# Ten products of a constant tile ahead of the first layer's cumulative sum, and dt's columns copied ahead of the SiLUs

## The chip, the cores and the metric

The kernel runs as one program on one core of one Trainium2 chip. The metric is the time of one execution on the device, in microseconds. The time before is the median of three runs: 20413.0 us (20402.2 to 20426.97).

## The reference

A network of two "metaformer" layers works on x, 8 images of 128 channels and 64 x 64 positions (4096 tokens an image), in float32. Layer 0 is a four-direction selective scan and a layer of 64 experts; it isn't touched. Layer 1's token mixer is what the change touches. It is a state-space model ("SSD") that is applied in three places:

```python
def _mamba(x, in_w, in_b, conv_w, conv_b, A_log, D, dt_bias, rms_w, out_w, headdim, d_state):
    zxbcdt = x @ in_w.T + in_b
    z, xBC = zxbcdt[..., :di], zxbcdt[..., di:2 * di + 2 * d_state]
    dt = softplus(zxbcdt[..., -nh:] + dt_bias)
    xBC = silu(causal_conv_of_3(xBC, conv_w) + conv_b)
    xs, Bm, Cm = xBC[..., :di], xBC[..., di:di + d_state], xBC[..., di + d_state:]
    y = _ssd(xs * dt, dt * -exp(A_log), Bm, Cm) + D * xs
    y = y * silu(z)
    return (y * rsqrt(mean(y * y) + 1e-5) * rms_w) @ out_w.T

# in the mixer of layer 1
gf  = _mamba(gf, sm_...) + gf                      # the seeds: 8 channels, all images
def cascade(xi):                                   # for each of 8 splits of 16 channels
    for i in range(2):
        xi = _mamba(xi, cm_in_w[i], ...)           # 4 heads of 8, state of 64
    return xi
ys = vmap(cascade)(xs) + xs * skip_scale
```

_ssd is the chunked form of the recurrence: within a chunk, decays exp(cs[l] - cs[s]) of the cumulative sum cs of dt * A weigh the products C[l]·B[s]; across chunks a state is carried.

## The kernel before, in words

The second half of the program has three stages one after another: the seeds (function seeds), the cascade (cascade), and a last stage with the layer's convolutions and experts (second_ffn). The names in the profile end in _sm for the seeds and in _cm for the cascade.

The cascade cuts each image into 16 segments of 256 tokens, 128 segments in all, and handles all 8 channel splits of a segment at once. A segment passes through both _mamba layers. In each of them it is *projected* (ssd_project), worked on in two *chunks* of 128 tokens (ssd_chunk) and put out (ssd_output). The loop `for n in range(total + 2)` has 130 turns. A turn interleaves by hand four chunks (both of segment n in layer 0, both of segment n - 2 in layer 1), the projection of segment n + 1 in layer 0, the projection of segment n - 1 in layer 1, and the outputs. The functions are generators; each yield is a place where the loop may go on with another one. The order thus written is the order in which instructions are given out; a scheduler settles the order on each engine[...].

A projection makes, in this order:
- bc_p: B and C, on TensorE, then one SiLU on ScalarE for each bank pair;
- z_p: z, and its SiLU;
- tok_p: x, B and dt with the tokens on the partitions, once for each of the two chunks. A bank pair holds both halves of a chunk's columns. For each half, ScalarE takes the SiLU of the first columns (tok_cm, row L284) and VectorE copies dt's 16 columns (dtr_cm, row L993);
- silus_done: a table load on ScalarE, behind all SiLUs, for exp and ln;
- dt by softplus: Abs, Exp and Ln on ScalarE (e_cm, e_cm, dt_cm), maximum, products and sums on VectorE (r_cm, tmp_cm, dt_cm), and dA = dt * A on VectorE;
- ssd_exponents: the cumulative sum cs_p on TensorE, which waits for dA; its three bf16 parts on VectorE (csq_cm, csr_cm), sent to memory and back as rows of the exponents by SyncE's transfers (cs_cm, ssA_cm, ssB_cm, csw_cm, eA_cm);
- dec_p and cd_p: the decays to a chunk's end, on TensorE, each with an Exp on ScalarE.

A chunk has g_p (C·B, TensorE) and gm_cm (its mask, VectorE), pad_cm, xw_cm and xD_cm (x with dt, with the decay and with D; the last on GpSimd), ss_p (the exponents, eight TensorE products of 512 columns), E_cm (their Exp, on ScalarE, then times gm on VectorE, row L332), yo_s_p (the state's part), S_cm (the new state; Sd_cm, its copy, on GpSimd), y_p (the sum, many small TensorE products), yy_cm and yz_cm. An output has sq_cm, o_p and rs_cm.

PSUM is given out in rings: tag "a" has 3 pairs of banks in the cascade (bc_p, z_p, tok_p, g_p, ss_p), tag "b" has 2 banks (cs_p, dec_p, cd_p, yo_s_p, y_p, o_p). A tile in a ring waits for the readers of the tile that had its place.

The seeds run the same ssd_project, ssd_chunk and ssd_output for 16 segments (all images at once), interleaved with the preparation of their inputs, and end each segment with det_p, eight TensorE products that wait for gf on VectorE.

ssd_weights makes the constants of one such layer: called for the cascade's layers 0 and 1 and for the seeds with index 0 (second_setup). mm, act, tt and ts (rows L281, L284, L323, L326 to L329) are the helpers that issue one instruction each, so many groups of the profile share a line and are told apart by the tiles.

Of the kernel before, what the change touches and what calls it, by code (L numbers as in the profile page):

```python
# [9 lines left out]
F32 = mybir.dt.float32  # L10
BF16 = mybir.dt.bfloat16
AF = mybir.ActivationFunctionType
# [11 lines left out]
S = 512  # L24
# [247 lines left out]
class Net:  # L272
# [6 lines left out]

    def mm(self, out, lhsT, rhs, start=True, stop=True):  # L280
        self.ordered(self.nc.tensor.matmul(out, lhsT=lhsT, rhs=rhs, start=start, stop=stop))  # L281

    def act(self, out, in_, func, **kw):
        i = self.ordered(self.nc.scalar.activation(out, in_, func, **kw))  # L284
# [562 lines left out]
    def ssd_weights(self, pool, cfg, j):  # L847

        nc = self.nc
        n = f"{cfg.name}{j}"  # L850

        def part(i):
            o, m = self.at["stacked"][f"{n}_{i}"]
            return self.st[:, o : o + m]

        W = pool.tile([128, cfg.cols], F32, name=f"W_{n}")
        nc.vector.memset(W[96:], 0.0)
        self.tt(W[:KST], part(0), part(1), ALU.mult)
        self.tt(W[:KST], W[:KST], part(2), ALU.add)
        negA = pool.tile([128, cfg.nh], F32, name=f"negA_{n}")  # L860
        self.act(negA, self.w(f"{n}_Alog"), AF.Exp)
        self.ts(negA, negA, -1.0, ALU.mult)
        D = pool.tile([128, cfg.g2, cfg.nh, cfg.hd], F32, name=f"D_{n}")
        for g in range(cfg.g2):
            nc.vector.tensor_copy(D[:, g], bc(self.w(f"{n}_D"), cfg.hd))
        wo = pool.tile([cfg.pz, cfg.gh * cfg.co], F32, name=f"wo_{n}")
        self.ts(wo, self.w(f"{n}_out")[: cfg.pz], self.w(f"{n}_rms")[: cfg.pz], ALU.mult)
        return {"W": W, "negA": negA, "D": D.rearrange("p g h q -> p (g h q)"), "wo": wo}

    def ssd_rings(self, pool, cfg, n, npads, nrows, nstates):  # L870

# [33 lines left out]
        ring[what] = (q + 1) % len(ring[what + "s"])  # L905
        return ring[what + "s"][q]

    def ssd_exponents(self, cfg, dA, n_tok, ring, wk, ps):


        nc = self.nc
        NC, nh, G = n_tok // 128, cfg.nh, cfg.g
        n = NC * G * nh
        t_ = cfg.name
        p = ps.tile([128, S], F32, tag="b", bufs=self.narrow, name="cs_p")
        p = p[:n, :128]
        self.mm(p, dA.rearrange("p c g -> p (c g)"), self.k("le"))
        part = wk.tile([n, 3, 128], BF16, name=f"csq_{t_}")
        rest = wk.tile([n, 128], F32, name=f"csr_{t_}")
        whole = wk.tile([n, 128], F32, name=f"csw_{t_}")  # L920
        nc.scalar.copy(whole, p)
        nc.vector.tensor_copy(part[:, 0], p)
        self.tt(rest, p, part[:, 0], ALU.subtract)
        nc.vector.tensor_copy(part[:, 1], rest)
        self.tt(part[:, 2], rest, part[:, 1], ALU.subtract)
        d = self.dp.tile([3, n, 128], BF16, name=f"cs_{t_}", bufs=3)
        nc.sync.dma_start(d.rearrange("i n t -> n i t"), part)
        A, B = self.turn(ring, "row")
        g4 = cfg.g4
        for r in range(g4):  # L930
            v = d.rearrange("i (c g h) t -> i c g h t", g=g4, h=nh)[:, :, r]
            nc.sync.dma_start(B[32 * r : 32 * r + 3], v)
            for i in range(3):
                o = 32 * r + 3 + i * nh
                nc.sync.dma_start(A[o : o + nh, :, r], v[i].rearrange("c h t -> h c t"))
        w = self.dp.tile([n, 128], F32, name=f"csw_{t_}", bufs=3)
        nc.sync.dma_start(w, whole)
        NH, m = cfg.nhalf, cfg.gh * nh
        eA = wk.tile([cfg.pz, NH, n_tok], F32, name=f"eA_{t_}", bufs=4 if cfg is CM else 3)
        for c in range(NC):  # L940
            for hf in range(NH):
                at = (c * NH + hf) * m
                nc.sync.dma_start(eA[:, hf, c * 128 : (c + 1) * 128], bc(w[at : at + m], cfg.hd, 1))
        return A, B, eA

    def ssd_project(self, cfg, W, ring, stk, n_tok, wk, ps):
# [3 lines left out]
        nc = self.nc  # L950
        NP, G, nh, hd, hi, ds = cfg.np, cfg.g, cfg.nh, cfg.hd, cfg.hi, cfg.ds
        g2, NH, gh, pb, pz = cfg.g2, cfg.nhalf, cfg.gh, cfg.pb, cfg.pz
        GH = G * nh
        NC = n_tok // 128
        t_ = cfg.name
# [8 lines left out]
        for j0 in range(0, NP, per):  # L964
            p = ps.tile([128, 2, S], F32, tag="a", bufs=self.wide, name="bc_p")
            v = p.rearrange("p a s -> p (a s)")[:pb, : per * 2 * n_tok].rearrange("p (j x s) -> p j x s", x=2, s=n_tok)
# [15 lines left out]
        nbk, ppb = NP // cfg.ppb, cfg.ppb  # L982
        for c in range(NC):
            p = ps.tile([128, 2, S], F32, tag="a", bufs=self.wide, name="tok_p")
            for j in range(NP):
                o = (j % ppb) * cfg.wtok
                self.mm(p[:, j // ppb, o : o + cfg.wtok], stk(j)[:, c * 128 : (c + 1) * 128],
                        Wp[:, cfg.o_t : cfg.o_t + cfg.wtok])
            for q in range(nbk):
                v = p[:, q, : ppb * cfg.wtok].rearrange("p (j f) -> p j f", j=ppb)  # L990
                jj = slice(q * ppb, (q + 1) * ppb)
                silus.append(self.act(tok[:, c, jj, :], v[:, :, : cfg.wsil], AF.Silu))
                nc.vector.tensor_copy(dtr[:, c, jj, :], v[:, :, cfg.wsil :])  # L993
            if c < NC - 1:
                yield None
        self.silus_done(silus)
        yield "silu"


        def small(name, bufs=2):  # L1000
            return wk.tile([128, NC, GH], F32, name=f"{name}_{t_}", bufs=bufs)

        dtr = dtr.rearrange("p c j f -> p c (j f)")
        e, r, tmp, dA = (small(n) for n in ("e", "r", "tmp", "dA"))
        dt, w = (small(n, nl_) for n in ("dt", "wd"))
        self.act(e, dtr, AF.Abs)
        self.ts(r, dtr, 0.0, ALU.max)
        self.softplus(dt, r, e, tmp, nc.vector)
        self.tt(dA.rearrange("p c (g h) -> p (c g) h", h=nh), dt.rearrange("p c (g h) -> p (c g) h", h=nh),
                bc(W["negA"], NC * G, 1), ALU.mult)  # L1010
        yield None
        ssA, ssB, eA = self.ssd_exponents(cfg, dA, n_tok, ring, wk, ps)
        yield None

        p = ps.tile([128, S], F32, tag="b", bufs=self.narrow, name="dec_p")
# [651 lines left out]
    def run(self, ctx):  # L1667
        tc, nc, nb = self.tc, self.nc, self.nb
        cp = ctx.enter_context(tc.tile_pool(name="cp", bufs=1))
        dp = ctx.enter_context(tc.tile_pool(name="dp", bufs=1, space=DRAM))  # L1670
        self.kt = cp.tile(list(self.A["const"].shape), F32, name="kt")
        nc.sync.dma_start(self.kt, self.A["const"])
        self.xs = [dp.tile([C, L], F32, name=f"xs_{b}") for b in range(nb)]
        self.ys = [dp.tile([C, L], F32, name=f"ys_{b}") for b in range(nb)]
        self.x1 = [dp.tile([C, L], F32, name=f"x1_{b}") for b in range(nb)]
        self.x2 = [dp.tile([C, L], F32, name=f"x2_{b}") for b in range(nb)]
        self.seed = [dp.tile([C, L], F32, name=f"seed_{b}") for b in range(nb)]
        self.P = [dp.tile([NE, L], F32, name=f"P_{b}") for b in range(nb)]
        self.dp = dp
        self.eo = cp.tile([NE, nb, C], F32, name="eo")  # L1680
        with tc.tile_pool(name="mid", bufs=1) as mp:
            self.pooled = mp.tile([C, NE, nb], F32, name="pooled")
            with tc.tile_pool(name="l0", bufs=1) as pl:
                self.scan_weights(pl)
                self.silus_done([])
                r = pl.tile([C, L], F32, name="r")
                for b in range(nb + 1):
                    with tc.tile_pool(name=f"in{b}", bufs=1) as rp, tc.tile_pool(name=f"inw{b}", bufs=2) as wk, \
                            tc.tile_pool(name=f"inps{b}", bufs=1, space=PSUM) as ps:
                        gens = []  # L1690
                        if b:
                            gens.append(self.route_tokens(b - 1, r, rp, wk, ps))
                        if b < nb:
                            xp, xt = (pl.tile([C, L + 2 * PAD], F32, name=n) for n in ("xp", "xt"))
                            gens.append(self.scan_inputs(b, r, xp, xt, wk, ps))
                        self.turns(*gens)
                    if b < nb:
                        self.first_mixer(b, r, xp, xt)
            self.experts()
        self.act_fence = self.act_exp = None  # L1700
        pl = ctx.enter_context(tc.tile_pool(name="l1", bufs=1))
        self.weights(pl, "second")
        with tc.tile_pool(name="l1s", bufs=1, space=PSUM) as ps:
            self.second_setup(pl, ps)
        self.seeds()
        with tc.tile_pool(name="l1b", bufs=4, space=PSUM) as ps:
            self.gms = pl.tile([C, nb, NSC], F32, name="gms")
            self.wide, self.narrow = 3, 2
            self.cascade(ps)
        self.second_ffn()  # L1710
# [23 lines left out]
```

## Time and profile before

| what | value |
|---|---|
| median of three runs | 20413.0 us (20402.2 to 20426.97) |
| the profiled execution, its own time | 20402.59 us |
| its span, first to last instruction | 20400.8 us |
| mean granted TensorE clock | 0.913 |
| busy: TensorE, its weight loads, VectorE, ScalarE, GpSimd | 80%, 40%, 76%, 55%, 41% |
| seeds, about 9930 to 10900 us: TensorE busy, clock | 754 of 970 us, 0.75 |
| cascade, about 10900 to 18800 us: TensorE busy, clock | 6815 of 7900 us, 0.91 |
| cascade: cs_p, waits for dA | 519.5 us in 113 of them, between 11000 and 18000 us |

A row of a view in order of time gives the start and the length in us, engine, line, operation, the tile written and the tiles read, the shapes and how many instructions the row holds; in brackets the idle time of the engine just before it and whom it waited for. A shape such as 128*64 before the operand of a product says how much of the 128 x 128 array it fills, rows by columns. A row of waits names who waited, for whom, for how long in total, how often and at most. PEclk in the line of slices is the granted TensorE clock in tenths.

### The profile page before, as it was taken

Reading aid. Unit: us, or ns where it says so; the run is one execution under the profiler, and the core shown is the slowest. Engines: PE = TensorE matmul, PEld = TensorE weight load, DVE = VectorE, ACT = ScalarE, POOL = GpSimd, SP = SyncE. Lnnn points to the kernel's source line nnn. Section 1 sums busy time; section 2 is a strip of 40 time slices with the busy share of each in tenths; the row PEclk is TensorE's granted clock in tenths of the full one; section 3 lists DMA queues with packets and bytes.
Section 4 is the critical chain, followed back from the end, with each engine's and each line's share of the span. In section 5 each row is a group of like instructions: output and inputs, shape, how many; then the busy total and the mean of one; then the engine's idle time right before and its main releaser. Section 6 shows DMA issues by size and latency. Waiting matters only on the chain. (4 is left out here: it accounts for less than half of the span.)

```text
span 20400.8 us, 305956 instructions
## 1 busy us (share of the span) xinstructions
PE 16385.0 (80%) x115485; PEld 8172.9 (40%) x115485; DVE 15587.1 (76%) x21096; ACT 11132.5 (55%) x15963; POOL 8451.5 (41%) x6020
## 2 busy tenths in 40 slices
PE   6777777777777777777877888888888888888899
PEld 2222222222222222223534555555555555555343
DVE  7989899898989989897454666666666666666886
ACT  5555555555555555554344555555555555555553
POOL 6767677686767767675110111111111111111444
PEclk9999899899989999998777999999999999998899
DMA  4445454454545445454431111111111111111222
GB/s 117 136 110 137 109 134 132 111 138 109 136 107 134 139 110 135 112 133 118 150 122 37 36 35 36 35 36 36 35 36 36 35 35 36 36 35 40 80 97 80
DMA packets 991471, 1764.26 MB, mean 86 GB/s; under 512 B 202091, under 2 KB 590603, under 8 KB 981067
## 3 DMA queue, kind: packets, MB, share of 16 engines
q1 hardware_dynamic: 989998, 1744.68, 30.6%
q8 instruction: 917, 15.02, 0.3%
q14 instruction: 556, 4.55, 0.1%
HBM read 1511.36 MB, written 232.91 MB: 86 GB/s over the span
## 5 line engine op out<-in xcount | busy, mean ns | idle before, releaser
L323 POOL TENSOR_TENSOR bx<-xE,B 128x1024 f32<-128x1024 f32 x2048 | 4823.6, 2356 | 1420.3 <-DMA xE<-dtx_d 1316.1
L281 PE MATMUL dA<-parts,expand 128*128 128x512 bf16 x12288 | 3194.7, 398 | 2076.4 <-DVE last L335 1525.7
L284 ACT ACTIVATE dA<-dA,negA 128x1024 f32<-128x1024 f32 x2048 | 2228.6, 1088 | 3665.1 <-PE dA L281 3627.7
L615 DVE TENSOR_TENSOR_SCAN dA<-dA,last,bx 128x1024 f32<-128x1024 f32 x1536 | 3610.7, 2351 | 172.5 <-POOL bx L323 165.1
L281 PEld LDWEIGHTS <-expand 128*128 128x128 bf16 x12288 | 1073.4, 100 | 4799.9 <-DVE last L335 2710.5
L332 DVE SCALAR_TENSOR_TENSOR E_cm<-E_cm,gm_cm 128x1024 f32<-128x1024 f32 x2048 | 2418.8, 1217 | 741.9 <-ACT E_cm L284 741.7
L284 ACT ACTIVATE E_cm<-ss_p 128x1024 f32<-128x1024 f32 x2048 | 1959.8, 1027 | 1139.2 <-PE ss_p L281 1137.8
L323 DVE TENSOR_TENSOR hc<-dA,C 128x1024 f32<-128x1024 f32 x2048 | 2508.4, 1225 | 70.0
L1128 POOL COPY Sd_cm<-S_cm 64x128 f32<-64x128 f32 x1024 | 331.7, 324 | 4528.5 <-DVE S_cm L323 4418.8
L323 POOL TENSOR_TENSOR xD_cm<-tok_cm,D_cm 128x256 f32<-128x256 f32 x512 | 525.4, 1026 | 2591.9 <-PE y_p L281 1865.0
L281 PE MATMUL y_p<-E_cm,pad_cm 128*32 128x128 f32 x32768 | 1338.2, 276 | 45.2 <-DVE E_cm L332 44.9
L615 DVE TENSOR_TENSOR_SCAN dA<-dA,bx 128x1024 f32<-128x1024 f32 x512 | 1173.2, 2291 | 187.6 <-POOL bx L323 186.2
L281 PE MATMUL ss_p<-ssB_cm,ssA_cm 128*128 128x512 bf16 x4096 | 1297.9, 430 | 22.8 <-DMA ssB_cm<-cs_cm 10.8
L281 PE MATMUL y<-hc,kt 128*32 128x512 f32 x8192 | 1187.7, 645 | 29.3 <-DVE hc L323 29.3
L281 PEld LDWEIGHTS y_p<-E_cm,pad_cm 128*32 128x32 f32 x32768 | 964.9, 110 | 290.4 <-DVE E_cm L332 180.6
L281 PE MATMUL bc_p<-stk_cm,W_cm 128*128 128x256 f32 x4096 | 1026.0, 394 | 47.8 <-DMA stk_cm<-xs 20.6
L281 PEld LDWEIGHTS bc_p<-stk_cm,W_cm 128*128 128x128 f32 x4096 | 740.6, 191 | 264.4 <-issue 97.8
L323 DVE TENSOR_TENSOR gm_cm<-g_p,kt 128x1024 f32<-128x1024 f32 x512 | 623.7, 1218 | 256.0 <-PE g_p L281 256.0
L284 ACT ACTIVATE tok_cm<-tok_p 128x384 f32<-128x384 f32 x1024 | 502.8, 491 | 538.6 <-PE tok_p L281 397.4
L281 PE MATMUL g_p<-BC_cm 64*128 64x128 f32 x8192 | 729.7, 296 | 83.0 <-ACT BC_cm L284 51.1
L281 PE MATMUL tok_p<-W_cm,stk_cm 128*128 128x200 f32 x4096 | 767.8, 341 | 0.0
L332 DVE SCALAR_TENSOR_TENSOR dw<-h,w_second,dw 128x512 f32<-128x512 f32 x1024 | 723.3, 748 | 1.5 <-ACT h L284 1.2
(388 smaller groups left out, 29223.5 us busy)
## 6 DMA issues: line engine op xcount, KB each, us to landing
xE<-dtx_d SPq DMA_DIRECT2D x2048, 512.0 KB
dtx_d<-dtx SPq DMA_DIRECT2D x256, 256.0 KB
eA_cm<-csw_cm SPq DMA_DIRECT2D x1024, 64.0 KB
pb<-p_d SPq DMA_DIRECT2D x64, 1024.0 KB
x<-x SPq DMA_DIRECT2D x192, 256.0 KB
ssA_cm<-cs_cm SPq DMA_DIRECT2D x3072, 4.0 KB
stk_cm<-xs SPq DMA_DIRECT2D x368, 128.0 KB
stk_cm<-y SPq DMA_DIRECT2D x368, 128.0 KB
```

Source lines behind the costliest of these rows:

```text
L281: self.ordered(self.nc.tensor.matmul(out, lhsT=lhsT, rhs=rhs, start=start, stop=stop))
L284: i = self.ordered(self.nc.scalar.activation(out, in_, func, **kw))
L323: self.ordered((eng or self.nc.vector).tensor_tensor(out, a, b, op))
L332: self.ordered(self.nc.vector.scalar_tensor_tensor(out=out, in0=a, scalar=s, in1=b, op0=op0, op1=op1))
L615: self.ordered(nc.vector.tensor_tensor_scan(out=t, data0=t, data1=bx.pop(n), initial=0.0 if ch["j"] == 0 else last[:, q : q + 1], op0=ALU. ...
L1128: nc.gpsimd.tensor_copy(Sd[gr, :, g * hi : (g + 1) * hi], S2[gr])
```

## The change

There are two edits. First, a helper keep_warm issues n products of a constant bf16 tile (128 x 128 weights against 512 columns, all ones) into the bank that the cumulative sum cs_p writes next; cs_p starts its own sum, so nothing of them stays. ssd_weights gives the number, `fill`: ten for index j = 0, that is for the cascade's first layer and for the seeds, none for the cascade's second layer. The tile, `warm`, is set once. Secondly, in ssd_project the copies of dt's columns of a bank pair are issued ahead of that pair's SiLUs, not each behind its own SiLU; and Abs is issued ahead of silus_done's table load, not behind it.

```diff
+    def keep_warm(self, bank, n):
+        for _ in range(n):
+            self.mm(bank, self.warm[:, :128], self.warm)
...
-        return {"W": W, "negA": negA, "D": D.rearrange("p g h q -> p (g h q)"), "wo": wo}
+        return {"W": W, "negA": negA, "D": D.rearrange("p g h q -> p (g h q)"), "wo": wo, "fill": 10 if j == 0 else 0}
...
-    def ssd_exponents(self, cfg, dA, n_tok, ring, wk, ps):
+    def ssd_exponents(self, cfg, dA, n_tok, ring, wk, ps, fill):
...
         p = ps.tile([128, S], F32, tag="b", bufs=self.narrow, name="cs_p")
+        self.keep_warm(p, fill)
         p = p[:n, :128]
         self.mm(p, dA.rearrange("p c g -> p (c g)"), self.k("le"))
...
-            for q in range(nbk):
-                v = p[:, q, : ppb * cfg.wtok].rearrange("p (j f) -> p j f", j=ppb)
-                jj = slice(q * ppb, (q + 1) * ppb)
+            banks = [(slice(q * ppb, (q + 1) * ppb),
+                      p[:, q, : ppb * cfg.wtok].rearrange("p (j f) -> p j f", j=ppb)) for q in range(nbk)]
+            for jj, v in banks:
+                nc.vector.tensor_copy(dtr[:, c, jj, :], v[:, :, cfg.wsil :])
+            for jj, v in banks:
                 silus.append(self.act(tok[:, c, jj, :], v[:, :, : cfg.wsil], AF.Silu))
-                nc.vector.tensor_copy(dtr[:, c, jj, :], v[:, :, cfg.wsil :])
             if c < NC - 1:
                 yield None
+        dtr = dtr.rearrange("p c j f -> p c (j f)")
+        e = wk.tile([128, NC, GH], F32, name=f"e_{t_}", bufs=2)
+        self.act(e, dtr, AF.Abs)
         self.silus_done(silus)
         yield "silu"
...
-        dtr = dtr.rearrange("p c j f -> p c (j f)")
-        e, r, tmp, dA = (small(n) for n in ("e", "r", "tmp", "dA"))
+        r, tmp, dA = (small(n) for n in ("r", "tmp", "dA"))
         dt, w = (small(n, nl_) for n in ("dt", "wd"))
-        self.act(e, dtr, AF.Abs)
         self.ts(r, dtr, 0.0, ALU.max)
...
-        ssA, ssB, eA = self.ssd_exponents(cfg, dA, n_tok, ring, wk, ps)
+        ssA, ssB, eA = self.ssd_exponents(cfg, dA, n_tok, ring, wk, ps, W["fill"])
...
         self.weights(pl, "second")
+        self.warm = pl.tile([128, S], BF16, name="warm")
+        nc.vector.memset(self.warm, 1.0)
```

On the engines, the changed program has 1440 more TensorE products (144 projections by ten) with a weight load each, one more memset, the same number of table loads, and the same order of SyncE's transfers. In 110 of the cascade's turns all ten fills stand between tok_p and cs_p of layer 0. In layer 0's half of a turn TensorE's yo_s_p now all stand ahead of the first ss_p, o_p stands between ss_p, and the first rs_cm of ScalarE stands behind the first E_cm.

## The prediction

> **What bounds the kernel now.** I read the page's busy table and slices first, then the same busy times cut by stage, then the waits of the cascade's stage, then one turn of it in order of time.
>
> ```profile
> PE   6777777777777777777877888888888888888899
> PEclk9999899899989999998777999999999999998899
> ```
>
> The second half of the run is TensorE's: 8 and 9 tenths busy. The granted clock is nine tenths there, with a dip to seven in the slices where the seeds run. By stage (0 to 9.7 ms the first mixers, then seeds, cascade, last stage):
>
> ```profile
> 9930.00:10900.00 970.00, 754.44 (x4287) 366.35 (x4286) 529.32 (x1082) 452.63 (x751) 137.37 (x218) 0.75 0.36 114
> 10900.00:18800.00 7900.00, 6814.94 (x79366) 4568.68 (x79368) 5144.77 (x10412) 4580.65 (x6881) 854.43 (x1530) 0.91 0.13 35
> ```
>
> The columns are length, busy time of PE, PE's weight loads, VectorE, ScalarE and GpSimd, the clock, the DMA share. The cascade takes 7900 us, 86% of it with TensorE busy. The change touches only it and the seeds (970 us, clock 0.75). The cascade's waits (total us, times, longest):
>
> ```profile
> DVE dtr_cm L993 <- ACT tok_cm L284: 563.1, 910, 17.0
> PEld cs_p L281 <- issue: 551.4, 114, 5.0
> PE cs_p L281 <- DVE dA_cm L323: 519.5, 113, 4.7
> ```
>
> Once a turn TensorE stands 4.6 us before cs_p, until VectorE has dA. One turn on TensorE:
>
> ```profile
> 14063.38 2.97 PE L281 MATMUL tok_p<-W_cm,stk_cm 128*128 128x200 f32 x16
> 14070.95 0.66 PE L281 MATMUL cs_p<-kt,dA_cm 128*64 128x128 f32 x2 [4.60 <-DVE dA_cm L323]
> 14072.59 0.69 PE L281 MATMUL dec_p<-dA_cm,kt 128*128 128x64 f32 x2 [0.98 <-DVE csr_cm L323]
> 14073.59 0.43 PE L281 MATMUL cd_p<-dA_cm,kt 128*64 128x32 f32 x4 [0.31 <-ACT wd_cm L284]
> 14074.41 1.09 PE L281 MATMUL yo_s_p<-BC_cm,Sd_cm 128*64 128x128 f32 x6 [0.39 <-ACT cd_cm L284]
> 14075.42 2.31 PE L281 MATMUL ss_p<-ssB_cm,ssA_cm 128*128 128x512 bf16 x5
> ```
>
> Call T the end of layer 0's tok_p, here 14066.35. The clock in consecutive stretches of that turn (same columns):
>
> ```profile
> 14062.60:14066.00 3.40, 3.40 (x31) 3.28 (x28) 1.85 (x4) 1.70 (x4) 0.31 (x1) 1.00 0.07 17
> 14066.00:14069.40 3.40, 0.35 (x3) 0.04 (x1) 0.72 (x4) 3.03 (x6) 0.00 (x0) 0.99 0.41 123
> 14069.40:14072.80 3.40, 0.87 (x3) 0.50 (x4) 1.88 (x8) 0.67 (x3) 0.00 (x0) 0.50 0.01 3
> 14072.80:14076.20 3.40, 2.70 (x14) 1.58 (x15) 0.51 (x2) 0.42 (x2) 0.00 (x0) 0.50 0.19 42
> 14076.20:14079.70 3.50, 3.50 (x24) 1.92 (x23) 1.73 (x3) 1.02 (x1) 0.15 (x1) 0.52 0.12 33
> 14079.70:14083.10 3.40, 3.07 (x50) 1.90 (x50) 2.55 (x4) 2.85 (x3) 0.56 (x2) 1.00 0.06 13
> ```
>
> The idle stretch is followed by three at half clock, in which dense work (yo_s_p, ss_p) runs at half speed; then full clock to the next turn. 116 of 152 half-clock stretches of the cascade last 10.24 us. The turns, T to T, have a mean of 61.40 us, and most are 61.44, exactly 18 times 3.413 us, the step in which the clock changes.
>
> [...] 1.00 and 0.50 alone, 10.24 us = 3 windows. [...] five ss_p span 2.31 us above, and 1.29 us at 14024.40 at full clock[...]. How busy a window must be the page doesn't say. I took it from the clock record: summing each window's products at full-clock cost, weighted by the rows and columns of the array they fill, windows below about 0.36 precede half clock and fuller ones mostly full. At half clock that takes an array about 72% filled all window.
>
> **The fills, cascade.** 128 projections of layer 0 get ten products of 512 columns: 10 x 0.216 = 2.16 us at full clock, 4.27 us at half. In 110 of 127 turns their place in TensorE's order is behind tok_p and ahead of cs_p. They wait for the bank's earlier reader, VectorE's yy of layer 1, which ends at 14062.43, before T. So they run T to T+2.2 in idle time that lasts to T+4.6. Cost on the path: nothing while cs_p is later than T+2.2 (or T+4.3 at half clock).
> Do they hold the clock? They leave T+2.2 to T+4.9 idle, and cs_p, dec_p and cd_p fill the array for only some 0.27 us by T+8. A window needs 0.36 x 3.41 = 1.23 us of work. One that begins later than T+0.95 has less than that of the fills; one that begins before about T+5.9 hasn't enough of yo_s_p and ss_p. This gap of 4.95 us is longer than a window, so one always begins in it. The clock still drops, only later: at T+4.4 to T+7.8 instead of T+1.2 to T+4.6. The dense part from T+8.1 then lies in the half-clock time as before. It lasts two windows where the second begins beyond about T+9, else three: its end is T+11.2 to T+15, before mostly T+11.4 to T+13.7.
>
> **dt's columns first.** Both copies of a bank pair (0.17 us each, row L993) now stand ahead of the pair's SiLUs (0.49 us each):
>
> ```profile
> 14065.83 1.05 ACT L284 ACTIVATE tok_cm<-tok_p 128x384 f32<-128x384 f32 x2 [0.24 <-DVE dtr_cm L993]
> 14067.12 0.49 ACT L284 ACTIVATE tok_cm<-tok_p 128x384 f32<-128x384 f32 x1 [0.24 <-DVE dtr_cm L993]
> ```
>
> Two gaps of 0.24 us go; in front of each of two pairs ScalarE now waits for two copies, about 0.4 us. From the end of tok_p: 0.45 + 2 x 0.49 = 1.43 us; before, the last SiLU ended 1.26 us behind it. With the handover I put the SiLUs' end 0.26 us later, and with it dA and cs_p (bounds -0.25, if the copies slip in beside tok_p, and +0.5). Abs (0.26 us) moves ahead of the table load (1.28 us). In layer 0 that is a mere swap. In layer 1 Abs stood behind four E_cm (row at 14107.43) and now stands ahead of them, so the first E_cm is 0.26 + 0.28 = 0.54 us later. VectorE's masked products and TensorE's ss_p and g_p queue behind it; g_p already waits 0.23 us for E_cm there (14043.59), so no slack covers it: +0.5 us a turn (bounds 0.2, as Abs is missing later, and 0.6). SP's transfers keep their order and GpSimd's queue is nearly the same.
> Layer 0's half is also reordered: all yo_s_p ahead of ss_p, o_p between the ss_p, rs behind the first E_cm on ScalarE (it waits for o_p, and the next E_cm behind it). I value that at nothing, bounds -0.3 and +0.5 us a turn.
>
> **The turn.** Over some 125 turns of before, a turn takes about 58.3 + 0.235 us for each us by which the half clock ends behind T (ends of 11.4 to 12.2 give 60.9 to 61.0; 13.2 to 13.7 give 61.45). After: 0.5 us from layer 1, less half-clock work because it starts later (-0.95 us for an end at T+12, -0.35 at T+13.5, +0.3 at T+14.7), gives 61.0 to 62.25 us by the phase. 61.44 lies inside. A turn over 61.44 brings the next half clock nearer to T, which shortens the next turn, and the reverse: turns settle at 18 windows again. Likeliest 0 us x 112 turns. Around the image borders 14 turns have 3 or 6 fills ahead of g_p or tok_p, where TensorE doesn't idle: 14 x about 5 x 0.216 = +15 us.
>
> **The seeds.** 16 fills of ten. In most segments 9 or 10 of them fall between o_p and det_p:
>
> ```profile
> 10720.91 2.07 PE L281 MATMUL det_p<-gf,w_seeds 64*128 64x256 f32 x4 [2.37 <-DVE gf L323]
> ```
>
> They need 2.16 us of a 2.37 us gap. In the last six segments the clock is half for over 40 us at a stretch, since det_p fills only 64 rows. Full-array fills may lift a window over 0.36: the eight rows of det_p and tok_p, some 12.7 us at half clock, would take about 7.5: -5 us x 6. In some seven earlier segments -1.5 to -3 us: about -15. Sum -45 us, bounds -70 and, if the fills run cold (4.27 us against 2.37), +15.
>
> **Sum.** 20402.6 (this execution; span 20400.8) - 45 + 15 = 20373. The runs' median lies 10.4 above this execution: 20383. A change within 0.2%, 41 us, can't be told from none here.
>
> **Rivals.**
> A, above: chance 0.54, 20383, own range 20345 to 20420.
> B, the turn leaves the lock upward (slower): the later E_cm and rs's wait for o_p, inside TensorE's full stretch from ScalarE's first E_cm of layer 1 on. It decides as soon as the shortest turn, 61.0 above, is over 61.44, so with 0.44 us more than I gave. Then turns average about 62.2: 0.75 x 125 = +94, so 20477. For it: no slack there. Against: Abs comes back later. Chance 0.23.
> C, below the lock: the 0.5 us is absorbed, and the later half clock saves more; 60.8 us or so, -0.65 x 125 = -80: 20303. Chance 0.12.
> D, the fills keep the full clock: seven or eight us of half-clock work run at full. By the fit above a turn without any is some 58.9 us: -2.5 x 125 = -310: 20073. Against: the gap of 4.95 us. It would hold if the three small products count by time, not by the array filled. Chance 0.06.
> E, no gain in the seeds and the lock: 20428, and with cold fills 20443. Chance 0.05.
>
> **Numbers.** The range leaves out D, some C below 20280 and B's upper part: 20280 to 20500. Faster: C, D, and a third of A, 0.37. Slower: nearly all of B and some of E, 0.25. Same: 0.38.
>
> **What would show it.** After cs_p's wait on dA the row should read about 2.7 us, with cs_p 0.26 us later behind T. PEclk should still show 0.50 in each turn, beginning near T+6; turns of 61.44 us mean A, of 62 B, of 59 D. dtr_cm's wait should be on TensorE, and g_p's on E_cm should grow by up to 0.5. Seeds' clock above 0.75 and a stage shorter by 45 us. Wrong if the half clock is gone, or the turns leave 61.44.

## The result and the profile after

The changed kernel takes 20240.6 us in the median (20234.4 to 20263.7, four runs) against 20407.6 us for the kernel before (four runs): 0.992, with an interval of 0.990 to 0.994. That is 167 us less. I had forecast 20383 us, and the time lies outside my range, below it.

The profiled execution took 20246.5 us (span 20244.5), 156.0 us less than the profiled one of before. By stage, from the first to the last TensorE instruction of each:

| stage | before | after | difference |
|---|---|---|---|
| all ahead of the seeds | 9946.3 us | 9934.1 us | -12.2 (code unchanged; 9901 to 9979 us in the traces of this study) |
| seeds | 924.2 us | 882.1 us | -42.1 |
| cascade | 7945.5 us | 7844.4 us | -101.1 |
| last stage | 1550.4 us | 1549.4 us | -1.0 |

The seeds gave about what I had forecast. The cascade, which I expected to stay, gave 101 us, and this is what the rest is about. (The rows of L284, L323 and L993 are L289, L328 and L998 in the changed kernel.) The slices of the page of after, first TensorE's busy share, then the clock:

```profile
PE   6777777777777777777887888888888888888899
PEclk9989999998999989899687999999999999998899
```

In tenths the clock looks as before. Cut by stage (length, busy PE, weight loads, VectorE, ScalarE, GpSimd, clock, DMA share and GB/s), seeds and then the same 7900 us of the cascade:

```profile
9930.00:10900.00 970.00, 776.03 (x4730) 382.28 (x4732) 536.52 (x1120) 466.44 (x779) 144.71 (x223) 0.79 0.35 113
10900.00:18800.00 7900.00, 6986.93 (x80834) 4642.07 (x80826) 5098.58 (x10530) 4552.23 (x6981) 882.98 (x1558) 0.94 0.13 36
```

The clock went from 0.75 to 0.79 and from 0.91 to 0.94. TensorE is busier and the stage is shorter all the same: part of what fills it are the fills, whose products nobody uses, and the rest runs faster. The waits of the cascade (11000 to 18000 us; total, times, longest):

```profile
ACT tok_cm L289 <- DVE dtr_cm L998: 527.6, 458, 2.5
...
DVE dtr_cm L998 <- PE tok_p L281: 325.3, 460, 1.1
...
ACT rs_cm L289 <- PE o_p L281: 273.3, 115, 3.1
PE cs_p L281 <- DVE dA_cm L328: 264.6, 117, 3.5
...
PE g_p L281 <- ACT E_cm L289: 104.8, 228, 0.6
```

cs_p's wait on dA halved (519.5 us before). Copies now wait for TensorE and SiLUs for copies, as the order asks. Two waits are new in size: ScalarE's rs_cm for o_p (1.3 us in all before), and g_p for E_cm (25.4 us before). One turn on TensorE; T, the end of tok_p, is 15239.97:

```profile
15237.00 2.97 PE L281 MATMUL tok_p<-W_cm,stk_cm 128*128 128x200 f32 x16
15239.81 2.32 PE L281 MATMUL cs_p<-warm 128*128 128x512 bf16 x10
15244.33 0.43 PE L281 MATMUL cs_p<-kt,dA_cm 128*64 128x128 f32 x2 [2.20 <-DVE dA_cm L328]
15245.83 0.41 PE L281 MATMUL dec_p<-dA_cm,kt 128*128 128x64 f32 x2 [1.08 <-DVE csr_cm L328]
15246.55 0.43 PE L281 MATMUL cd_p<-dA_cm,kt 128*64 128x32 f32 x4 [0.31 <-ACT wd_cm L289]
15247.37 1.12 PE L281 MATMUL yo_s_p<-BC_cm,Sd_cm 128*64 128x128 f32 x8 [0.39 <-ACT cd_cm L289]
15248.25 1.04 PE L281 MATMUL yo_s_p<-xw_cm,tok_cm 128*64 128x32 f32 x16
15249.22 2.31 PE L281 MATMUL ss_p<-ssB_cm,ssA_cm 128*128 128x512 bf16 x5
...
15255.62 0.60 PE L281 MATMUL g_p<-BC_cm 64*128 64x128 f32 x6 [0.60 <-ACT E_cm L289]
```

cs_p stands at T+4.36, not T+4.60 as before nor T+4.86 as I had it. The fills are the row cs_p<-warm. cs_p and dec_p take 0.43 and 0.41 us (0.66 and 0.69 before): they run at full clock now. yo_s_p begins at T+7.40 instead of T+8.06. In both traces the granted clock is only ever 1.00 or 0.50, and it changes on a grid of 3.413 us (836 stretches before, 818 after, every edge within 0.03 us of the grid); a window, below, is one step of that grid. The fills follow each other every 216 ns at 1.00 and every 427 ns at 0.50 (medians of 1191 and 24 in the trace of after). The same turn cut at the clock's steps (columns as above):

```profile
15239.40:15242.90 3.50, 2.73 (x14) 1.22 (x12) 0.45 (x3) 3.01 (x7) 0.00 (x0) 1.00 0.42 119
15242.90:15246.30 3.40, 0.84 (x4) 0.49 (x4) 2.16 (x9) 0.67 (x4) 0.00 (x0) 1.00 0.00 0
15246.30:15249.70 3.40, 2.76 (x30) 2.32 (x31) 0.60 (x3) 0.40 (x2) 0.03 (x1) 0.50 0.26 63
15249.70:15253.10 3.40, 3.40 (x10) 0.82 (x8) 2.10 (x4) 1.02 (x1) 0.69 (x2) 0.50 0.06 14
15253.10:15256.50 3.40, 2.80 (x25) 1.43 (x24) 0.90 (x1) 2.32 (x4) 0.00 (x0) 1.00 0.07 17
```

The idle window is there as forecast, the second row; but only two windows of half clock follow it, where three did before. Over all turns, means from the two traces:

| per turn of the cascade | before | after |
|---|---|---|
| turn, T to T | 61.47 us (mostly 61.4) | 60.69 us (59.4 to 62.2) |
| half clock | 9.95 us | 6.11 us |
| half-clock stretches of 10.24 / 6.83 / 3.41 us | 102 / 15 / 5 | 1 / 89 / 25 |
| T to cs_p | 4.60 us | 4.36 us |
| cs_p to yo_s_p | 3.43 us | 3.13 us |
| T to the end of layer 1's tok_p | 33.95 us | 33.09 us |
| from there to the next T | 27.52 us | 27.60 us |

All of the gain lies in the part of the turn that begins with the fills. Turns with one half-clock window take 59.7 us on average, those with two 61.0.

### The profile page after: what moved, and what is told of

Same layout as the page of the kernel before. It is cut to its first block, busy times and chain, and to the rows that moved or that the text cites. A ratio compares the mean times of both kernels' runs of the same rounds, so it can differ in the third digit from the quotient of the medians.

```text
span 20244.5 us, 309615 instructions
## 1 busy us (share of the span) xinstructions
PE 16480.4 (81%) x116925; PEld 8220.9 (41%) x116925; DVE 15464.5 (76%) x21097; ACT 11037.6 (55%) x15963; POOL 8453.6 (42%) x6020
## 5 line engine op out<-in xcount | busy, mean ns | idle before, releaser
L328 POOL TENSOR_TENSOR bx<-xE,B 128x1024 f32<-128x1024 f32 x2048 | 4819.6, 2354 | 1406.3 <-DMA xE<-dtx_d 1291.1
L289 ACT ACTIVATE dA<-dA,negA 128x1024 f32<-128x1024 f32 x2048 | 2228.6, 1088 | 3657.9 <-PE dA L281 3616.2
L328 DVE TENSOR_TENSOR hc<-dA,C 128x1024 f32<-128x1024 f32 x2048 | 2507.5, 1224 | 69.9
L289 ACT ACTIVATE E_cm<-ss_p 128x1024 f32<-128x1024 f32 x2048 | 1971.1, 1026 | 858.6 <-PE ss_p L281 857.2
L328 POOL TENSOR_TENSOR xD_cm<-tok_cm,D_cm 128x256 f32<-128x256 f32 x512 | 526.1, 1028 | 2913.6 <-PE y_p L281 2134.5
L281 PE MATMUL ss_p<-ssB_cm,ssA_cm 128*128 128x512 bf16 x4096 | 1256.6, 420 | 18.8 <-DMA ssB_cm<-cs_cm 12.0
L328 DVE TENSOR_TENSOR gm_cm<-g_p,kt 128x1024 f32<-128x1024 f32 x512 | 623.9, 1219 | 248.8 <-PE g_p L281 248.8
L289 ACT ACTIVATE tok_cm<-tok_p 128x384 f32<-128x384 f32 x1024 | 446.5, 488 | 586.1 <-DVE dtr_cm L998 584.6
```

Source lines behind the costliest of these rows:

```text
L328: self.ordered((eng or self.nc.vector).tensor_tensor(out, a, b, op))
```

## The experiments

Each edit is against the changed kernel, and each ratio against the kernel before, measured in the same group of runs. "Turn" and "half clock" are means from the run's trace.

**e1, no fills.** In ssd_weights:

```diff
-        "fill": 10 if j == 0 else 0
+        "fill": 0
```

> The changed kernel without any fills: dt's columns ahead of the SiLUs and Abs ahead of the table load alone. Clock theory (the fills shorten the half clock of each turn from about 10 to about 6 us, and that is the cascade's gain): cs_p 0.24 us earlier behind T, half clock again near 10 us a turn, turns of 61.2 to 61.5 us, seeds 924 us as before: 20370 to 20410 us. Order theory (the cascade's gain comes from cs_p's earlier start and the shorter ScalarE chain): turns near 60.8 us, so 20280 to 20310 us.

Measured: 20387.4 us, ratio 0.999 (0.998 to 1.000). Turn 61.47 us, half clock 9.88, cs_p at T+4.45. The new order of copies and Abs shortens the chain to cs_p by 0.15 us here and leaves the turn where it was. The order theory falls for ScalarE and VectorE. TensorE's own order (yo_s_p, ss_p, o_p) is close to that of before in this run; e3 and e7 test it.

**e2, the fills alone.** dt's copies go back behind their SiLUs, and Abs behind silus_done:

```diff
-            for jj, v in banks:
-                nc.vector.tensor_copy(dtr[:, c, jj, :], v[:, :, cfg.wsil :])
             for jj, v in banks:
                 silus.append(self.act(tok[:, c, jj, :], v[:, :, : cfg.wsil], AF.Silu))
+                nc.vector.tensor_copy(dtr[:, c, jj, :], v[:, :, cfg.wsil :])
...
-        self.act(e, dtr, AF.Abs)
         self.silus_done(silus)
...
+        self.act(e, dtr, AF.Abs)
         self.ts(r, dtr, 0.0, ALU.max)
```

> The ten fills alone, with dt's columns and Abs where they were before. In about half of the turns only 6 of the ten fills now stand behind tok_p, in the other half 9. Clock theory: half clock 6 to 8 us a turn, cs_p 4.6 us behind T, no later E_cm in layer 1: turns near 60.8 us, seeds 882 us: 20250 to 20300 us. Order theory: the turns stay near 61.4 us and only the seeds gain: 20350 to 20370 us.

Measured: 20321.2 us, 0.995 (0.994 to 0.997). Half clock 6.68 us, but the turn only fell to 61.29 us; the seeds took 878 us. Neither theory hit. cs_p stands at T+4.50, 0.10 us earlier than before. From T to the end of layer 1's tok_p the turn takes 33.36 us, 0.59 less than before; from there to the next T it takes 27.92, 0.40 more. So the part with the shorter half clock did gain, and the other took most of it back. In that other part some of the fills now stand in front of g_p, and TensorE waits 0.37 us a turn ahead of them, for yy_cm on VectorE; but e10 (below) has the same wait and doesn't lose there, so what lengthens that part in e2 stays open.

**e3, thin fills.** The same instructions in the same order, each working 1/16 of the array:

```diff
-            self.mm(bank, self.warm[:, :128], self.warm)
+            self.mm(bank[:32], self.warm[:32, :32], self.warm[:32])
```

> The changed kernel, every instruction in the same place, but each fill uses 32 x 32 of the array instead of 128 x 128, with the same 512 columns and so the same duration. If the clock counts the array filled (as my threshold did): half clock back to about 10 us a turn, turns 61.3 to 61.5 us, seeds 924 us: 20360 to 20400 us. If the clock counts TensorE's busy time, whatever it fills, or if the gain is the order of instructions: as the changed kernel, turns 60.7 us; 20240 us (time), or with the seeds lost 20285 us (order).

Measured: 20387.5 us, 0.998 (0.997 to 0.999). Turn 61.44 us, half clock 9.68 us. A turn of e3 on TensorE:

```profile
14049.22 2.33 PE L281 MATMUL cs_p<-warm 32*32 32x512 bf16 x10
14053.64 0.69 PE L281 MATMUL cs_p<-kt,dA_cm 128*64 128x128 f32 x2 [2.10 <-DVE dA_cm L328]
```

The fills last 2.33 us, as the full ones do (2.32), but cs_p takes 0.69 us: half clock again. So it isn't TensorE's busy time that keeps the clock up here, nor the order of the instructions, but how much of the array the fills work; with that, nearly the whole of the cascade's gain goes. Rows and columns were cut together, so this run doesn't tell which of them counts. The seeds took 901 us, between 926 (e1) and 882 us, and their half clock fell from 473 us (e1) to 394 (349 with full fills). So in the seeds more than half of the gain stays with thin fills, which the array's work doesn't explain.

**e4, fills in the seeds alone.**

```diff
-        "fill": 10 if j == 0 else 0
+        "fill": 10 if cfg is SM else 0
```

> The changed kernel with the fills in the seeds alone, none in the cascade. My step of the seeds (-45 us by the clock there): 40 to 45 us below the run without any fill, seeds stage 882 us. Rival: the seeds' 42 us came with the order of dt's columns, so no difference to the run without any fill.

Measured: 20334.8 us, 0.996 (0.994 to 0.997), 53 us below e1. By the stage in the traces 891 us against 926: 35 us. The forecast of 40 to 45 lies between the two, and the rival falls: it is the fills, not dt's columns, that shorten the seeds. Turn 61.47 us.

**e5, twenty fills; e7, five fills** in the cascade's first layer, ten in the seeds.

```diff
-        "fill": 10 if j == 0 else 0
+        "fill": (10 if cfg is SM else 20) if j == 0 else 0
```

> The changed kernel with twenty fills instead of ten in the cascade's first layer (the seeds keep ten). Twenty at full clock take 4.3 us, just what stands between tok_p and cs_p. If the gap without array work is what drops the clock, no window is left that is idle enough, except around dec_p and cd_p: half clock 0 to 3.4 us a turn, turns of 58.9 to 59.8 us (the changed kernel's turns with one window of half clock took 59.5): 20020 to 20130 us. Rival: fills that meet a half clock take 8.5 us and push cs_p back by 4 us, so turns of 62 to 64 us: 20450 us or more.

Measured: 20013.2 us, 0.981 (0.978 to 0.983). Turn 58.68 us, half clock 1.29 us. The cascade of e5 in a cut of 7500 us, clock 0.99 (third number from the end):

```profile
10900.00:18400.00 7500.00, 6932.29 (x81656) 4615.36 (x81654) 5009.29 (x10377) 4491.43 (x6856) 940.37 (x1523) 0.99 0.13 37
```

The time lies just under the forecast. In 86 of the 121 turns that are not at the cascade's ends there is no half clock at all, and these take 58.01 us in the median (mean 58.17). That is near 17 windows (58.03), but in a turn without half clock the clock can't be what holds it: it is the turn's own length at full clock, 0.7 us under the 58.9 us that I had put on it.

> The changed kernel with five fills instead of ten in the cascade's first layer (the seeds keep ten). By the threshold of 0.36 a window needs 1.23 us of full-clock work; five fills have 1.08 us, so only windows that also catch the end of tok_p are lifted. Clock theory: half clock between 6.1 and 9.9 us, near 8 us a turn, turns 61.0 to 61.4 us: 20290 to 20330 us. Rival (the order that the scheduler makes with fills is the gain; it is the same here): turns 60.7 us, 20240 us.

Measured, with five: 20361.0 us, 0.997 (0.996 to 0.999). Turn 61.38 us (spread 0.25), half clock 10.0 us, with the order on TensorE and cs_p (T+4.36) of the changed kernel. Not even the part of the half clock that I expected is saved, and the turn stands at 18 windows. What the run gains on e1 is the seeds' (873 us). The order isn't the gain here either.

**e6, nineteen fills ahead of cs_p and three ahead of dec_p.**

```diff
-        "fill": 10 if j == 0 else 0
+        "fill": (10 if cfg is SM else 19) if j == 0 else 0
...
+        if cfg is CM:
+            self.keep_warm(p, W["fill"] // 5)
         self.mm(p[:, : NC * GH], self.k("gt"), dA.rearrange("p c g -> p (c g)"))
```

> Nineteen fills ahead of cs_p and three more ahead of dec_p, in each turn's first layer; in the second layer none; the seeds keep ten ahead of cs_p and get two ahead of none. TensorE has then no stretch of over 0.7 us without work between tok_p and the dense part. Clock theory: full clock throughout, turns near 58.9 us: 20000 to 20050 us. Rival: what the clock gains is lost, since layer 1's half of the turn is VectorE's and ScalarE's (10 tenths busy): turns not under 60 us, 20150 us or more.

Measured: 20138.3 us, 0.987 (0.985 to 0.989). Turn 59.93 us, half clock 1.87. Between theory and rival, and worse than twenty fills without the bridge. TensorE in e6:

```profile
14065.13 0.82 PE L281 MATMUL dec_p<-warm 128*128 128x512 bf16 x3 [0.98 <-DVE csr_cm L328]
14065.79 0.33 PE L281 MATMUL dec_p<-dA_cm,kt 128*128 128x64 f32 x2
```

The three fills write dec_p's bank, and so they wait for the same csr_cm that dec_p waits for. They don't fill the wait; they stand behind it and push dec_p back by 0.66 us. A fill must be free to start when the gap opens. The scheduler also set most of yo_s_p behind the first ss_p, and about every other turn still had one window of half clock.

**e8, Abs behind the table load; e10, Abs ahead of it in layer 0 and the seeds only.** e8 puts Abs back as in e2; e10 is

```diff
-        self.act(e, dtr, AF.Abs)
+        if W["fill"]:
+            self.act(e, dtr, AF.Abs)
         self.silus_done(silus)
...
+        if not W["fill"]:
+            self.act(e, dtr, AF.Abs)
         self.ts(r, dtr, 0.0, ALU.max)
```

> The changed kernel with Abs behind the table load again, dt's columns still ahead of the SiLUs, ten fills. My step that Abs ahead of the table load costs layer 1: g_p's wait for E_cm falls from 1.2 by 0.25 to 0.3 us a turn. What I overlooked, that it shortens layer 0's chain: cs_p goes back from 4.36 to about 4.6 us behind T. Together within 0.2 us a turn: 20220 to 20260 us. If the Abs was the whole of the 0.56 us that g_p waits longer: turns 60.2 us, 20180 us.

Measured: 20280.6 us, 0.994 (0.992 to 0.996), turn 60.77 us, cs_p at T+4.49, half clock 7.03 us. The time is above the forecast. So Abs ahead of the load is worth 0.13 us of cs_p in layer 0. The 1.2 us of the expectation are all of g_p's waits; those for E_cm are 0.91 us a turn, and fall to 0.53. Only 0.09 of that fall is in layer 1's part of the turn.

> The changed kernel with Abs ahead of the table load in layer 0 and in the seeds alone; in the cascade's layer 1 it stands behind it, as before. In 108 turns 9 of the ten fills stand behind tok_p. My step of layer 1: g_p's wait for E_cm falls from 1.2 to about 0.9 us a turn and cs_p stays at T+4.36, so turns of 60.4 us: 20190 to 20230 us. Rival: E_cm isn't on the path, as the turn is given by the clock's windows: 20240 us.

Measured: 20230.3 us, 0.991 (0.990 to 0.993), turn 60.56 us. It can't be told from the changed kernel (0.990 to 0.994). g_p's wait for E_cm in layer 1's part is 0.23 us, as before the change, and that part of the turn takes 27.43 us instead of 27.59.

**e9, cs_p later; e15, cs_p and layer 1's E_cm later.** e9 puts back the first of two terms that I had too long, e15 a part of the second as well. e9:

```diff
+        if cfg is CM and W["fill"]:
+            for _ in range(2):
+                self.act(e, e, AF.Abs)
         self.softplus(dt, r, e, tmp, nc.vector)
```

> The changed kernel with Abs taken twice more in layer 0 of the cascade, behind the table load, which leaves its values as they are and puts cs_p some 0.55 us later, at T+4.9, where my prediction had it. On TensorE o_p now stands behind the eight ss_p again. If the turn left the lock at 18 windows because cs_p came 0.5 us earlier than I had it: turns settle at 61.4 us again, 20310 to 20350 us. If the lock was left because the half clock is shorter than I had it, wherever cs_p stands within half a microsecond: turns near 61.0 us (60.7 and some 0.3 to 0.5), 20270 to 20300 us.

Measured: 20294.9 us, 0.995 (0.993 to 0.996). cs_p at T+4.93, turn 61.01 us, half clock 6.83 us. The turn grew by 0.3 us and did not go back to 61.44, as the second of the two cases in the expectation has it. e15 adds one more Abs, written ahead of layer 1's table load:

```diff
         self.act(e, dtr, AF.Abs)
+        if cfg is CM and not W["fill"]:
+            self.act(e, e, AF.Abs)
         self.silus_done(silus)
```

> The run with the later cs_p (Abs twice more in layer 0, cs_p at T+4.93), and Abs once more ahead of the table load in the cascade's layer 1, which puts the first E_cm there some 0.43 us later than in the kernel before, near the 0.54 us that I had forecast. Order of TensorE as in the run with the later cs_p. If the lock at 18 windows was missed because I had these two terms 0.5 and 0.4 us too long: turns settle at 61.4 us, 20320 to 20350 us. If it is missed because the half clock wakes earlier than I had it: turns still under 61.3 us, some of them with a single window, 20290 to 20320 us.

Measured: 20319.2 us, 0.997 (0.995 to 0.998). Turn 61.23 us, half clock 6.77. ScalarE in layer 1's part of a turn of e15:

```profile
14004.83 0.87 ACT L289 ACTIVATE tok_cm<-tok_p 128x384 f32<-128x384 f32 x2 [0.46 <-DVE dtr_cm L998]
14005.58 0.26 ACT L289 ACTIVATE e_cm<-dtr_cm 128x64 f32<-128x64 f32 x1
14005.86 1.28 ACT L320 ACT_TABLE_LOAD   x1
14007.15 0.26 ACT L289 ACTIVATE e_cm<-e_cm 128x64 f32<-128x64 f32 x1
14007.32 2.83 ACT L289 ACTIVATE E_cm<-ss_p 128x1024 f32<-128x1024 f32 x3
```

The added Abs ended up behind the load, and the first E_cm begins only 0.31 us later than in the kernel before, not 0.43 as expected nor 0.54 as predicted. So cs_p is put back in full and E_cm in part, and with that 0.54 of the 0.75 us between 60.69 and 61.44 are gone. Whether the rest is the missing 0.23 us of E_cm or the half clock, these runs don't tell. In both the turn isn't held at 61.44 (of the 121 turns 13 and 14 lie within 0.15 us of it; in the kernel before it is 58). Both also have yo_s_p, ss_p and o_p in another order than the changed kernel, without its wait of 0.6 us for E_cm in layer 0, so the shares are rough.

**e11, twenty fills with e10's edit.**

> Twenty fills with Abs ahead of the table load in layer 0 alone. With twenty fills most turns took 58.0 us, 17 windows of the clock. If the turn is held there by the windows, the 0.3 us that layer 1 gets back changes nothing: 20000 to 20020 us. If the turn follows its longest chain: 57.7 us, 19970 us.

Measured: 20019.9 us, 0.981 (0.980 to 0.983), the time of e5 within the noise. The turns without half clock (81 of 121) take 57.86 us in the median, against 58.01 in e5. So the 17 windows don't hold the turn; some of what layer 1 gets back shows there, but it is too little to show in the time.

**e12, thirty fills; e13, thirty thin fills; e14, forty fills.** The number as in e5, and for e13 the edit of e3.

> Thirty fills in the cascade's first layer. At full clock they take 6.5 us and put cs_p at T+6.6, 2.2 us later than it could start; the scheduler now puts five ss_p ahead of dec_p. Clock theory: no half clock but a later chain: turns of 58.7 + 2.2, less what the earlier ss_p fills, near 60 us: 20180 us. Rival: the chain behind cs_p is hidden behind other work, turns stay at 58 to 58.7 us: 20010 us.

Measured: 19860.4 us, 0.973 (0.971 to 0.975): the fastest kernel of the study. Turn 57.41 us, half clock 0.03 us a turn. A turn of e12 on TensorE (one of the thirty fills is missing from the trace):

```profile
13485.85 6.64 PE L281 MATMUL cs_p<-warm 128*128 128x512 bf16 x29
13492.42 0.43 PE L281 MATMUL cs_p<-kt,dA_cm 128*64 128x128 f32 x2
13492.78 1.25 PE L281 MATMUL ss_p<-ssB_cm,ssA_cm 128*128 128x512 bf16 x5
13493.92 0.41 PE L281 MATMUL dec_p<-dA_cm,kt 128*128 128x64 f32 x2
```

Both expectations missed, on the low side. cs_p comes 2 us later, but the scheduler now puts five ss_p between cs_p and dec_p, where TensorE stood idle 1.08 us, and the clock stays full.

> Thirty fills of 32 x 32 of the array: the order on TensorE and the length of the fills are those of the run with thirty whole fills, but they hardly work the array. If the clock is the gain: half clock of about 10 us a turn again, at which thirty fills take up to twice as long and cs_p comes even later: turns of 61.4 us (18 windows) or more, 20390 us or more. If the order (ss_p ahead of dec_p) is the gain: turns under 59 us, near 20000 us.

Measured: 20403.7 us, 1.000 (0.999 to 1.001), with the same order on TensorE. Turn 61.64 us, half clock 10.45 us, cs_p at T+7.98. The thin fills run at half clock in part, so cs_p comes 1.6 us later than in e12. The order gains nothing where the clock isn't kept up; the whole gain of e12 needs the array's work.

> Forty fills: 8.6 us at full clock, cs_p at T+8.6 or later, 4.3 us later than it could start. If the work behind cs_p is hidden (thirty fills delayed cs_p by 2 us and the turn became shorter), turns stay near 57.4 us: 19860 us. If ten more fills are now on the path, they cost 2.16 us a turn: 59.5 us, 20130 us. I expect between, 19950 us.

Measured: 20100.1 us, 0.986 (0.984 to 0.988), turn 59.59 us, clock 1.00 in the cascade. That is near the case of ten more fills on the path, 240 us more than e12. But it isn't a test of it, since TensorE has another order. A turn of e14, whose T is at 14002.2:

```profile
14003.72 6.86 PE L281 MATMUL cs_p<-warm 128*128 128x512 bf16 x31 [0.37 <-DVE yy_cm L328]
14010.42 1.24 PE L281 MATMUL ss_p<-ssB_cm,ssA_cm 128*128 128x512 bf16 x5
...
14014.82 0.43 PE L281 MATMUL cs_p<-kt,dA_cm 128*64 128x128 f32 x2
```

Twenty of yo_s_p's products stand ahead of the fills and eight ss_p between them, and cs_p comes at T+12.6, not T+8.6. Forty fills are worse than thirty; how much of that is the fills' length and how much the order stays open.

## Why the prediction was wrong

**Right.** The fills leave a window with too little array work in every turn (under 0.36 of a window by my sum ahead of each of the 248 half-clock windows of the changed kernel's cascade), and the clock still drops, in 126 of 126 turns of the trace; the half clock begins at T+3.3 to T+7.8, mostly T+5.2 to T+7.0 (forecast T+4.4 to T+7.8). The seeds: -42 us by the traces (forecast -45), and e1 and e4 show that it is the fills. There det_p in the last segments stands behind fills instead of an idle gap, and four of its products take 1.13 us instead of 2.07, at full clock:

```profile
10729.76 2.12 PE L281 MATMUL cs_p<-warm 128*128 128x512 bf16 x9
10732.19 1.13 PE L281 MATMUL det_p<-gf,w_seeds 64*128 64x256 f32 x4 [0.32 <-DVE gf L328]
```

But my reason there, array work that lifts a window over 0.36, is shown only in part: with thin fills (e3) more than half of the gain stays. So the right number for the seeds is in part luck.

The turn does hold to 18 windows where the half clock is long: in five kernels (before, e1, e3, e4, e7) it averages 61.38 to 61.48 us, though cs_p differs among them by 0.24 us and g_p's wait by half a microsecond, and in each about half of the turns or more lie within 0.15 us of 61.44 (12 of 121 in the changed kernel).

**The step that failed** is "The turn": "gives 61.0 to 62.25 us by the phase. 61.44 lies inside." The turns came at 59.4 to 62.2 us, with a mean of 60.69. By the forecast's own argument they settle at 61.44 only where some phase of the windows makes them that long; 109 of 121 were shorter. The sum had +0.5 us for layer 1 and -0.95 to +0.3 us for the half clock, and it would have needed about -0.5 there for 61.44. The table above has the two parts apart: the part with layer 1's E_cm grew by 0.08 us, not 0.5, and the part with the half clock shrank by 0.86 us, near the far end of what I had allowed. The terms behind them:

- *dt's columns and Abs in layer 0*: +0.26 us forecast for cs_p, -0.24 measured. I added up the lengths of single instructions. On ScalarE, after:

```profile
15239.02 0.87 ACT L289 ACTIVATE tok_cm<-tok_p 128x384 f32<-128x384 f32 x2 [1.77 <-DVE dtr_cm L998]
15240.36 0.87 ACT L289 ACTIVATE tok_cm<-tok_p 128x384 f32<-128x384 f32 x2 [0.46 <-DVE dtr_cm L998]
15241.11 0.26 ACT L289 ACTIVATE e_cm<-dtr_cm 128x64 f32<-128x64 f32 x1
15241.39 1.28 ACT L320 ACT_TABLE_LOAD   x1
```

Two SiLUs of 0.49 us take 0.87 us together, not 0.98, and Abs begins 0.12 us before the SiLUs' row ends. The last SiLU ends 1.26 us behind T, just as before; so dt's columns changed nothing in this chain. Activations that follow each other overlap by 0.11 to 0.12 us here, which I had not used. Abs ahead of the load costs the chain 0.14 us, not its 0.26: the load begins 0.16 us behind the last SiLU's end (15241.39), and 0.02 us behind it before. Behind the load Abs took 0.29. That makes dA 0.15 us earlier. The other 0.09 us of the 0.24 is the handover from dA's end to cs_p: 0.15 us before and in e1 and e4, 0.06 us or less with fills ahead of cs_p, be they ten, five or thin. I had no term for it, and why it is shorter no run shows.
- *Abs in layer 1*: +0.5 us forecast. The first E_cm begins 1.45 us behind the last SiLU instead of 1.31, so 0.14 us later and not 0.54, for the same reason, and g_p's wait for it grew from 0.23 to 0.32 us a turn. e10 takes this back, and layer 1's part gets 0.16 us shorter.
- *The half clock*: three or two windows forecast with an end at T+11.2 to T+15; two or one came, with ends mostly at T+10.1 to T+13.5. I kept yo_s_p at T+8.1 or later, "in the half-clock time as before", though a clock that drops later leaves cs_p and dec_p at full clock: yo_s_p begins mostly at T+7.3 to T+7.7, and a window of half clock that begins at T+6.7 to T+7.1 already holds enough dense work to be the last one (24 of 24 in the trace of after, none of 27 before). The threshold of 0.36 was my estimate from the clock record of before. Summed by array work (0.42 ns for a bf16 column and 0.84 for an f32 one, from 216 ns for 512 and for 256 columns at full clock, by the part of the array filled), 0.36 tells the next window's clock there in all but 5 of the cascade's 2314 windows. Whether it was too high for waking up stays open: in the changed kernel's cascade, 12 of the 134 half-clock windows that full clock follows lie below it, down to 0.33, and one of the 113 that half clock follows is at 0.35.

e9 puts back the first term (60.69 to 61.01 us): so cs_p's place alone isn't why the turn left 61.44. e15 puts back a part of the second as well (61.23). For the third, e2 comes nearest: with E_cm as before and cs_p only 0.10 us earlier than before, the part with the half clock is 0.59 us shorter. No run changes it alone, so the shares of the three in the 0.75 us are not settled.

**What I valued at nothing** was not: rs_cm behind the first E_cm makes g_p of layer 0 wait 0.60 us a turn for the next E_cm (row at 15255.62), 0.1 beyond my bound of +0.5. It didn't decide, as that part of the turn got shorter all the same; how much of the wait reaches the turn no run shows. In e5, with o_p behind the ss_p again, that wait is 0.07 us.

**The rivals.** C, below the lock, was the case (60.8 us; 60.69 came), at a chance of 0.12; I priced it at 20303 us, with the +15 us of the image borders in it. Its reason held in half: the later half clock saves more, but the 0.5 us were not absorbed, they hardly arose. The +15 us don't show: the cascade's 101 us are 5 more than 0.78 us times 123 turns. B's mechanism, a late E_cm without slack, is real (e15 against e9: 0.2 us for 0.16 us of delay) but its size was wrong. D needs more fills than ten, and its 58.9 us, which the fit doesn't give (58.3 for a half clock that ends at T), were high: turns without half clock take 58.2 us on average in e5 and 57.4 in e12.

Still open: how far the new order of yo_s_p, ss_p and o_p by itself helps or hurts when the turn is not locked. e3 and e13 show it worth nothing at half clock, where the lock can hide a few tenths of a microsecond; with full fills every run that went beyond ten changed the order too.

## What to carry to other kernels

In these runs a filler for the clock was worth the array work that it put into each window of the clock (thirty full fills 0.973, thirty thin ones 1.000), and only as far as few windows were left without (half clock 6.11 us a turn with ten, 1.29 with twenty, 0.03 with thirty): look at the time from its end to the next dense work, not only at its own length. Ten fills of 2.2 us in a gap of 4.6 us gave 0.8%, twenty gave 1.9%, thirty, which even delayed the next product by 2 us, 2.7%; forty gave 1.4%. Try the thin variant of a filler (same instructions, a sixteenth of the array) beside it: it separates the clock from the order that the filler also changes. Look in the trace where the scheduler has put what you added: in e14 and e15 it was not where it was meant to be. And where a short chain of small instructions decides, price it by the spacing of instructions that follow each other, not by the sum of their lengths.

## What the runs showed of the hardware that I had not expected

- In the cascade it is the part of the array in use that keeps the clock up, not busy time: ten fills of 32 x 32 last as long as ten of 128 x 128 (2.33 and 2.32 us) and keep next to nothing up (half clock 9.68 against 6.11 us a turn; 9.95 before). Thirty of them gave 1.000, thirty full ones 0.973. In the seeds the thin ones did shorten the half clock (473 to 394 us), and that stays open.
- A loop whose turn depends on the clock can settle at whole windows of it: 61.44 us (18 of 3.413) in five kernels. There some tenths of a microsecond on the chain vanish: e1 had cs_p 0.15 us earlier and took the same turn.
